# Attention and mixture of experts on one core: turning and first products of the normalised rows in halves of 64

## The chip, the cores and the metric

The kernel runs on one core of a Trainium2 chip. The metric is the device time in microseconds, as the median of several runs; a profiled execution gives one more time and a trace. The engines are named PE (matrix products and transposes), PEld (PE's loading of the stationary operand, which can overlap its products), DVE (vector), ACT (scalar), POOL and SP (which here starts most transfers).

## The reference, cut to what matters

```python
x = L0_attn_x                          # (2, 4096, 512) float32
xn = _layernorm(x, axis=-1)
x = x + attention(xn) + moe(xn)

# attention: causal, 64 wide, from a compressed row
c = (xn @ W_to_kv.T) @ W_compress.T    # 64 wide; then a layernorm, q, k, v, rope, softmax, output
# moe: 16 experts, 2 per token, and a shared one
router_logits = xn @ router_w.T        # 16 wide; softmax, top 2
shared = (silu(xn @ shared_gate_w) * (xn @ shared_up_w)) @ shared_down_w
```

All arithmetic is in float32. There are 8192 tokens of width 512. The change concerns how `xn` is transposed and how the 16 router logits and the 64 compressed values of each token are computed from the transposed rows.

## The kernel before, in words

The work has three phases. The first goes through 16 groups of 512 tokens (the list `seq`, which alternates between the two sequences of the batch): normalise, transpose, router logits and compressed values, the shared expert, and after every second group the projection to q, k and v. The second runs attention in part and the routed experts, the third the rest of attention with the sums of all parts. Only the first phase is touched. The second and third have their order on PE, DVE and ACT written out by hand (from L863); in the first phase the order on each engine is set by a scheduler when the kernel is built, which follows the program's order, but lets a later instruction pass an earlier one that isn't ready.

A group's steps, in program order:

- `front` (L341) makes `xn` from the rows `xt`: statistics on DVE, a root on ACT, four scalings on DVE (L350). It is called through `ahead()` (L436) in the middle of the group before, so the next `xn` is there early. Then POOL adds the output bias to `xt` (L353); the group's results are added to `xt` later.
- `group` (L397) transposes `xn` into `xnT`: for each of four column blocks `c`, four transposes of 128 x 128 (L402) into a bank of pool B, and one copy to `xnT`, three on ACT and one on DVE (L403).
- `plc` (L404 to L409): for each of four row blocks `i`, four products over `c` with `RC`, the router and compressing weights side by side (80 columns), summed in one bank, O. In the trace each float32 product is two passes, each with its own weight load. DVE copies the logits to `lg` (L411), takes statistics of the 64 compressed values (L415, L416), scales them into `cn` (L420), and finds the top two experts (L425, L426). The two weights go into two extra columns of `xn`, which SP stores to `xn_d` (L437).
- The shared expert's gate and up products, `gu` (L306, called by `product`), are a seven-product scheme of quarters of the matrices: `moved` (L286) makes sums of quarters of `xnT` on DVE, in place for one of them; each product fills a pair of banks of pool A and is taken into sums by ACT or DVE (L471 to L488).
- The down product, `pd`, has seven products too, in the order 1, 2, 4, 6, 7, 5, 3. Their banks alternate (L513): 1, 6 and 3 in T, 2 and 5 in O, 4 and 7 in half of a pair of A. DVE adds each to `xt` (`onto_x`, L521). The last lines are quoted below. SP stores `xt` to `acc_d` (L540).
- After each group of the second sequence, `project` (L546) transposes `cn` into a B bank (`ptc`), scales it into `chT` on DVE, and computes q and k (`qk`, two A pairs, L560; DVE multiplies by the rope table, L562; POOL adds, L563) and v (`pv`, an A pair, L568). Its products have 64 summands, with the two sequences in the two halves of the partitions.

PSUM has eight banks here: A two pairs, B two, O one and T one.

```python
                c5 = summed(5)
                V.tensor_tensor(m2, m2, c5, ALU.add)
                onto_x(1, 1, c5)
                onto_x(1, 1, m3)
                onto_x(1, 0, m3)
                onto_x(0, 1, summed(3))
                onto_x(0, 1, m2)
```

Of the kernel before, what the change touches and what calls it, by code (L numbers as in the profile page):

```python
# [8 lines left out]
F32 = mybir.dt.float32  # L9
# [3 lines left out]
ALU = mybir.AluOpType  # L13
# [6 lines left out]
P = 128  # L20
# [8 lines left out]
DC = 64  # L29
NE, FE, FS = 16, 256, 512  # L30
# [22 lines left out]
def tile_mla_then_moe(  # L53
# [23 lines left out]
    mm, tr = nc.tensor.matmul, nc.tensor.transpose  # L77
    V, S, G = nc.vector, nc.scalar, nc.gpsimd
# [13 lines left out]
    def psA(name):  # L92
        return ps.tile([P, 2, 512], F32, tag="A", name=name)

    def psB(name):
        return ps.tile([P, 512], F32, tag="B", name=name)

    def psO(name, second=False):
        return ps.tile([P, 512], F32, tag="T" if second else "O", name=name, bufs=1)
# [3 lines left out]
    def kept(shape, dtype, name):  # L103
        return keep.tile(shape, dtype, tag=name, name=name)


    ident = kept([P, P], F32, "ident")
# [167 lines left out]
    def quarter(t, i, j):  # L275
        return t[:, 2 * i:2 * i + 2, j * 256:(j + 1) * 256]
# [23 lines left out]
    def product(pieces, n):  # L300

        for o, fac in pieces:
            lhs, rhs = fac[n]
            for r in range(2):
                for c in range(2):
                    mm(out=o[:, r, :], lhsT=lhs[:, c, r * P:(r + 1) * P], rhs=rhs[:, c, :],  # L306
                       start=c == 0, stop=c == 1)


    with tc.tile_pool(name="p1w", bufs=1) as pw:  # L310
        gam = pw.tile([P, 1], F32, name="gam")
        bet = pw.tile([P, 1], F32, name="bet")
        RC = pw.tile([P, 4, NE + DC], F32, name="RC")
# [9 lines left out]
        with tc.tile_pool(name="p1", bufs=2) as p1:  # L323
# [11 lines left out]
            def rstd_of(mv, n, name):  # L335
                r = p1.tile([P, n], F32, tag="rstd", name=name, bufs=4)
                S.activation(r, mv[:, :, 1], AF.Sqrt, bias=eps_t)
                V.reciprocal(r, r)
                return r

            def front(g, xt):  # L341
                st = p1.tile([P, 4, 6], F32, tag="st", name=f"st{g}")
                mv = p1.tile([P, 4, 2], F32, tag="mv", name=f"mv{g}")
                for i in range(4):
                    V.bn_stats(st[:, i, :], xt[:, i, :])
                    V.bn_aggr(mv[:, i, :], st[:, i, :])
                r = rstd_of(mv, 4, f"rx{g}")
                xn = p1.tile([P, 4, D + TOPK], F32, tag="xn", name=f"xn{g}", bufs=1)
                for i in range(4):
                    V.tensor_scalar(xn[:, i, 0:D], xt[:, i, :], mv[:, i, 0:1], r[:, i:i + 1],  # L350
                                    ALU.subtract, ALU.mult)

                G.tensor_tensor(xt, xt, b_bc.unsqueeze(1).to_broadcast([P, 4, D]), ALU.add)  # L353
                return (xn,)
# [3 lines left out]
            def rank_of(g, idx8):  # L358
# [35 lines left out]
                            in_=tok[:, g * 4 + i, k:k + 1], in_offset=None)  # L394
                ranked.append(scatter)

            def group(g, xt, xn, cn, ahead):  # L397
                xnT = p1.tile([P, 4, 512], F32, tag="xnT", name=f"xnT{g}", bufs=1)
                for c in range(4):
                    pt = psB(f"pt{g}_{c}")  # L400
                    for i in range(4):
                        tr(pt[:, i * P:(i + 1) * P], xn[:, i, c * P:(c + 1) * P], ident)  # L402
                    (V.tensor_copy if c == 3 else S.copy)(xnT[:, c, :], pt)  # L403
                plc = psO(f"plc{g}")  # L404
                lc = plc.rearrange("p (i f) -> p i f", f=P)
                for i in range(4):
                    for c in range(4):
                        mm(out=lc[:, i, 0:NE + DC], lhsT=xnT[:, c, i * P:(i + 1) * P], rhs=RC[:, c, :],
                           start=(c == 0), stop=(c == 3))  # L409
                lg = p1.tile([P, 4, NE], F32, tag="lg", name=f"lg{g}")  # L410
                V.tensor_copy(lg, lc[:, :, 0:NE])  # L411
                st = p1.tile([P, 4, 6], F32, tag="st", name=f"stc{g}")
                mv = p1.tile([P, 4, 2], F32, tag="mv", name=f"mvc{g}")
                for i in range(4):
# [9 lines left out]
                for i in range(4):  # L424
# [11 lines left out]
                nxt = ahead()  # L436
                nc.sync.dma_start(  # L437
                    out=xn_d[g * 512:(g + 1) * 512, :].rearrange("(i p) d -> p i d", p=P), in_=xn
# [77 lines left out]
                def summed(n):  # L516
                    t = banks[n](f"pd{n}_{g}").rearrange("p (r d) -> p r d", r=2)
                    product([(t, fac_d)], n)
                    return t

                def onto_x(i, j, t):  # L521
                    xq = quarter(xt, i, j)
                    V.tensor_tensor(xq, xq, t, ALU.add)
# [11 lines left out]
                onto_x(1, 1, c5)  # L535
                onto_x(1, 1, m3)
                onto_x(1, 0, m3)
                onto_x(0, 1, summed(3))
                onto_x(0, 1, m2)
                nc.sync.dma_start(  # L540
                    out=acc_d[g * 512:(g + 1) * 512, :].rearrange("(i p) d -> p i d", p=P), in_=xt
# [30 lines left out]
            seq = [b * GPB + h for h in range(GPB) for b in range(NB)]  # L572
# [30 lines left out]
            pt = psB("pt_rw")  # L603
# [3 lines left out]
            pt = psB("pt_wcm")  # L607
            tr(pt[:, 0:DC], wcm, ident[:DC, :DC])
            V.tensor_copy(wcmT, pt[:, 0:DC])
            pt = psB("pt_wc")  # L610
            for c in range(4):
                mm(out=pt[:, c * DC:(c + 1) * DC], lhsT=wtk[:, c * P:(c + 1) * P], rhs=wcmT,
                   start=True, stop=True)
# [27 lines left out]
                    nc.sync.dma_start(out=order_d[t].rearrange("(p f) o -> p (f o)", p=P), in_=kc_z)  # L641

            cur = (x_first, *front(seq[0], x_first))
            cn = None
            for n, g in enumerate(seq):

                def ahead(n=n):
                    if n + 1 == len(seq):
                        return None
                    t = load_x(seq[n + 1])  # L650
                    return (t, *front(seq[n + 1], t))

                if g < GPB:
                    cn = p1.tile([P, 4, NB, DC], F32, tag="cn", name=f"cn{g}")
                cur = group(g, *cur, cn, ahead)
                if g >= GPB and g != seq[-1]:
                    project(g - GPB, cn)
                while ranked:
                    ranked.pop()()
# [507 lines left out]
```

## Time and profile before

| what | us |
|---|---|
| median of 3 runs | 2021.14 (2018.82 to 2023.4) |
| profiled execution | 1979.99 |
| its span | 1977.8 |
| PE busy in the span | 1898.8 (96%) |
| DVE busy | 1073.7 (54%) |
| ACT busy | 626.8 (32%) |
| transposes of `xn`, L402, in PE time | 40.2 (x256) |
| `plc`, L408, in PE time | 64.6 (x512 passes) |

The time of the profiled execution is its span and 2.2 us around it. It is one execution; the runs of the median are others. Busy times of PE are the sum of overlapping passes as the profile models them, so what a pass costs is read from the distance between starts, not from its duration: a merged group's length, less one duration, over the number of steps between. In a timeline, "x8" is eight merged instructions, and the bracket is the idle time of the engine before them and who ended it. "128*64 64x128"-like entries give rows times columns of the array, then the operand's partitions and elements.

### The profile page before, as it was taken

The page shows a single profiled execution, that of the slowest core. Times are in us where ns is not written, and L with a number is a line of the kernel's source. Part 1 is how long each engine was busy: PE and PEld are TensorE (multiplying, and loading weights), DVE is VectorE, ACT ScalarE, POOL GpSimd, SP SyncE. Part 2 cuts the span into 40 slices and gives each one's busy share as a digit, 9 for nine tenths or more (in the row PEclk, how much of TensorE's full clock was granted, in tenths as well). Part 3 has the DMA queues.
Part 4 walks back from the last instruction along what each step waited for, and adds up shares of the span by engine and source line. Part 5 has one row for each costly group of instructions (what it writes and reads, how often), then busy time and mean ns, then how long its engine had stood idle before and what let it go on. Part 6 is the DMA issues. An engine that isn't in the chain of part 4 may idle for free. (4 is left out here: it accounts for less than half of the span.)

```text
span 1977.8 us, 31805 instructions
## 1 busy us (share of the span) xinstructions
PE 1898.8 (96%) x12210; PEld 1407.1 (71%) x12210; DVE 1073.7 (54%) x2910; ACT 626.8 (32%) x1045; POOL 572.0 (29%) x499
## 2 busy tenths in 40 slices
PE   7999999999999988899999999999999999999997
PEld 6888888888888865467777777777777675444453
DVE  8878777787778766632222222222222324777775
ACT  2222222223222213541111111111111355576663
POOL 2333333323233341111111111111111104555554
PEclk9999999999999988999999999999999999999998
DMA  6122222222222213138788887877887776888887
GB/s 233 65 76 65 75 86 76 97 86 75 64 75 65 75 43 123 33 102 278 250 279 282 272 276 264 293 270 264 277 279 245 245 240 187 208 200 212 200 207 181
DMA packets 219434, 342.40 MB, mean 173 GB/s; under 512 B 19204, under 2 KB 109952, under 8 KB 219280
## 3 DMA queue, kind: packets, MB, share of 16 engines
q1 hardware_dynamic: 167600, 234.09, 36.4%
q0 software_dynamic: 31696, 69.99, 14.1%
q10 hardware_dynamic: 19984, 36.25, 4.8%
q8 instruction: 98, 1.61, 0.3%
q14 instruction: 56, 0.46, 0.1%
HBM read 250.22 MB, written 90.05 MB: 172 GB/s over the span
## 5 line engine op out<-in xcount | busy, mean ns | idle before, releaser
L995 PE MATMUL pg<-xt,wgu 128*128 128x256 f32 (+1 forms) x2816 | 496.1, 335 | 0.0
L995 PEld LDWEIGHTS pg<-xt,wgu 128*128 128x128 f32 x2816 | 434.8, 191 | 43.0 <-issue 0.5
L917 POOL DMA_INDIRECT xg<-xn_d,table x137 | 130.8, 955 | 685.5 <-DVE sw L977 553.0
L1001 DVE TENSOR_TENSOR eh<-esg,pg 128x512 f32<-128x512 f32 (+1 forms) x69 | 47.2, 684 | 396.6 <-ACT esg L1000 396.6
L1009 PE MATMUL py<-wdn,eh 128*128 128x512 f32 x548 | 247.1, 594 | 0.0
L972 DVE COPY xt<-pxt 128x512 f32<-128x512 f32 x138 | 88.3, 682 | 176.7 <-PE pxt L969 176.5
L1009 PEld LDWEIGHTS py<-wdn,eh 128*128 128x128 f32 x548 | 102.2, 190 | 106.6 <-issue 98.5
L742 ACT ACTIVATE E<-E,nb 128x1024 f32<-128x1024 f32 (+7 forms) x160 | 160.4, 1004 | 42.0 <-DVE nb L737 39.4
L1013 ACT ACTIVATE y<-py,sw 128x512 f32<-128x512 f32 x137 | 94.2, 688 | 231.1 <-PE py L1009 200.2
L734 DVE TENSOR_SCALAR_CACHE_REDUCE E<-s 128x512 f32<-128x512 f32 x224 | 143.5, 686 | 43.3 <-PE s L726 32.4
L1000 ACT ACTIVATE esg<-pg 128x512 f32<-128x512 f32 (+1 forms) x69 | 41.0, 594 | 382.8 <-PE pg L995 322.7
L726 PE MATMUL s<-kT,qT 64*128 64x512 f32 (+3 forms) x576 | 143.2, 595 | 11.4 <-DVE E L734 7.3
L392 POOL DMA_INDIRECT order_d<-tok,at_u x128 | 129.3, 1010 | 64.4 <-issue 36.4
L796 PE MATMUL oT<-eT,vv 128*64 128x256 f32 x1088 | 146.2, 391 | 0.4 <-DVE eT L782 0.2
L776 PEld LDWEIGHTS et<-ident,E 64*128 64x128 f32 x2112 | 81.7, 141 | 81.6 <-issue 50.1
L782 ACT COPY eT<-et 128x512 f32<-128x512 f32 x186 | 102.1, 586 | 102.9 <-PE et L776 66.3
L796 PEld LDWEIGHTS oT<-eT,vv 128*64 128x64 f32 x1088 | 67.3, 138 | 91.6 <-issue 35.3
L776 PE MATMUL et<-ident,E 64*128 64x64 f32 x2112 | 103.9, 233 | 26.0 <-ACT eT L782 15.4
L1084 POOL DMA_INDIRECT fac<-y_d,pos_all x64 | 98.8, 1544 | 71.3 <-DMA fac<-y_d,pos_all 56.4
L353 POOL TENSOR_TENSOR x<-x,b_bc 128x2048 f32<-128x2048 f32 x16 | 76.1, 4754 | 147.3 <-DVE xn L350 134.6
L1084 POOL DMA_INDIRECT fyy<-y_d,pos_all x64 | 82.7, 1292 | 114.0 <-ACT eT L782 54.2
L306 PE MATMUL gu<-xnT,Wg 128*128 128x256 f32 x384 | 98.5, 391 | 6.3 <-DVE ft L185 3.3
(241 smaller groups left out, 2782.4 us busy)
## 6 DMA issues: line engine op xcount, KB each, us to landing
wgu<-in_L_ffn_gate_w_dram SPq DMA_DIRECT2D x88, 512.0 KB, 6.0
wgu<-in_L_ffn_up_w_dram SPq DMA_DIRECT2D x88, 512.0 KB, 8.5
wdn<-in_L_ffn_down_w_dram SPq DMA_DIRECT2D x88, 512.0 KB, 4.1
y_d<-y ACTq DMA_DIRECT2D x137, 256.0 KB, 6.2
xn_d<-xn SPq DMA_DIRECT2D x16, 1028.0 KB, 4.9
x<-in_L_attn_x_dram SPq DMA_DIRECT2D x16, 1024.0 KB, 6.6
acc_d<-x SPq DMA_DIRECT2D x16, 1024.0 KB, 5.2
fac<-acc_d SPq DMA_DIRECT2D x64, 256.0 KB, 4.9
```

The lines of the kernel that those rows point to most:

```text
L306: mm(out=o[:, r, :], lhsT=lhs[:, c, r * P:(r + 1) * P], rhs=rhs[:, c, :], start=c == 0, stop=c == 1)
L392: G.indirect_dma_start(out=order_d[n % 4], out_offset=bass.IndirectOffsetOnAxis(ap=at_u[:, i, k:k + 1], axis=0), in_=tok[:, g * 4 + i, k:k ...
L726: mm(out=sc[b][:, 0:w], lhsT=q[e, :], rhs=kT[c][e, 0:w], start=True, stop=True)
L734: V.tensor_scalar(dst, sc[b][:, 0:w], SCALE, None, ALU.mult, ALU.max, accum_out=m)
L742: S.activation(E, E, AF.Exp, bias=nb[:, b:b + 1], accum_out=sm[:, b, c:c + 1])
L776: tr(pt[h][:, o:o + H], rows[i][j // 8][e, b, (j % 8) * P:(j % 8 + 1) * P], ident[e, e])
L782: copy(dst[:, h:h + 3:2, :], pt[h].rearrange("p (u c) -> p u c", u=2))
L796: mm(out=o, lhsT=vv[j // 4][:, b, j % 4, :], rhs=e, start=(j == 0), stop=(j == n - 1))
L917: G.indirect_dma_start(out=x_n, out_offset=None, in_=xn_d, in_offset=bass.IndirectOffsetOnAxis(ap=table[:, n:n + 1], axis=0))
L995: mm(out=pg[:, g, f, at_s], lhsT=weights[u][0][:, c, g * FE + f * P:g * FE + (f + 1) * P], rhs=x_u[:, c, :], start=(c == 0), stop=(c == 3))
L1009: mm(out=py[:, v, :], lhsT=hT[:, c, v * P:(v + 1) * P], rhs=weights[u][1][:, c, :], start=(c == 0), stop=(c == 1))
L1084: G.indirect_dma_start(out=y, out_offset=None, in_=y_d, in_offset=bass.IndirectOffsetOnAxis(ap=pos[k][:, j:j + 1], axis=0), compute_op=ALU ...
```

## The change

A new function `turn_x` transposes the next group's `xn`. It is called in `group` just ahead of the last down product (`pd3`), and once ahead of the loop. Each 128-row transpose becomes two of 64 rows, one per half `h` of the partitions, and each half has its own bank: two banks of B for the first two column blocks, one pair of A for the other two. Four copies, all on ACT, put the halves side by side in `xnT`.

The products with `RC` are split over the summands: partitions 0 to 63 into bank O, 64 to 127 into bank T, alternating. ACT copies the first bank to `lc0`, DVE adds the second to it into `lc`, in SBUF. The logits are a view of `lc`; statistics and scaling read `lc` where they read the bank.

```diff
+            turned = {}
+
+            def turn_x(g, xn):
+                xnT = p1.tile([P, 4, 512], F32, tag="xnT", name=f"xnT{g}", bufs=1)
+                for c2 in (0, 2):
+                    if c2:
+                        pair = psA(f"pt{g}_{c2}")
+                        pt = [pair[:, h, :] for h in range(2)]
+                    else:
+                        pt = [psB(f"pt{g}_{c2}_{h}") for h in range(2)]
+                    pt = [t.rearrange("p (c i q) -> p c i q", c=2, i=4) for t in pt]
+                    for c in range(2):
+                        for i in range(4):
+                            for h in range(2):
+                                e = slice(h * 64, (h + 1) * 64)
+                                tr(pt[h][:, c, i, :], xn[e, i, (c2 + c) * P:(c2 + c + 1) * P], ident[e, e])
+                    for h in range(2):
+                        S.copy(xnT[:, c2:c2 + 2, :].rearrange("p c (i h q) -> p c i h q", i=4, h=2)[:, :, :, h, :], pt[h])
+                turned[g] = xnT
+
             def group(g, xt, xn, cn, ahead):
-                xnT = p1.tile([P, 4, 512], F32, tag="xnT", name=f"xnT{g}", bufs=1)
-                for c in range(4):
-                    pt = psB(f"pt{g}_{c}")
-                    for i in range(4):
-                        tr(pt[:, i * P:(i + 1) * P], xn[:, i, c * P:(c + 1) * P], ident)
-                    (V.tensor_copy if c == 3 else S.copy)(xnT[:, c, :], pt)
-                plc = psO(f"plc{g}")
-                lc = plc.rearrange("p (i f) -> p i f", f=P)
+                xnT = turned.pop(g)
+                pl = [psO(f"plc{g}_{h}", h == 1).rearrange("p (i f) -> p i f", f=P) for h in range(2)]
                 for i in range(4):
                     for c in range(4):
-                        mm(out=lc[:, i, 0:NE + DC], lhsT=xnT[:, c, i * P:(i + 1) * P], rhs=RC[:, c, :],
-                           start=(c == 0), stop=(c == 3))
-                lg = p1.tile([P, 4, NE], F32, tag="lg", name=f"lg{g}")
-                V.tensor_copy(lg, lc[:, :, 0:NE])
+                        for h in range(2):
+                            e = slice(h * 64, (h + 1) * 64)
+                            mm(out=pl[h][:, i, 0:NE + DC], lhsT=xnT[e, c, i * P:(i + 1) * P], rhs=RC[e, c, :],
+                               start=(c == 0), stop=(c == 3))
+                lc0 = p1.tile([P, 4, NE + DC], F32, tag="lc0", name=f"lc0{g}", bufs=1)
+                lc = p1.tile([P, 4, NE + DC], F32, tag="lc", name=f"lc{g}", bufs=1)
+                S.copy(lc0, pl[0][:, :, 0:NE + DC])
+                V.tensor_tensor(lc, lc0, pl[1][:, :, 0:NE + DC], ALU.add)
+                lg = lc[:, :, 0:NE]
...
                 onto_x(1, 0, m3)
+                if nxt is not None:
+                    turn_x(seq[seq.index(g) + 1], nxt[1])
                 onto_x(0, 1, summed(3))
...
             cur = (x_first, *front(seq[0], x_first))
+            turn_x(seq[0], cur[1])
```

## The prediction

> **What bounds the kernel now.** I first read the busy times by stretch, since the change lives in the first phase only (it ends near 745 us; the weights of the last `gu` products that read `xnT` are loaded at 751.7 us). The columns are stretch, length, then busy time (and count) of PE, PE's weight loads, DVE, ACT, POOL, the granted clock and DMA.
>
> ```profile
> core 0: us, PE busy (x) PEld busy (x) DVE busy (x) ACT busy (x) POOL busy (x), PEclk, DMA share, GB/s
> ...
> 200.00:300.00 100.00, 98.49 (x540) 83.55 (x537) 76.27 (x191) 27.82 (x38) 34.76 (x30) 1.00 0.27 86
> 300.00:400.00 100.00, 98.79 (x526) 85.71 (x526) 79.62 (x227) 29.30 (x41) 30.71 (x26) 1.00 0.24 79
> ```
>
> PE is busy 98 to 99% at full clock; DVE follows at 76 to 80%, ACT has room (29%), DMA too. So a microsecond less on PE counts, as long as DVE keeps up. The matching waits of PE itself from 60 to 700 us name hardly anything but the transposes waiting for their banks (`PE pt L402 <- ACT xnT L403`, 6.4 us in 14 waits). "Busy" hides more than that, though, because matmul ends are modelled; so next I read PE's weight loads in order of time (start, duration from first to last of the merged group), at a group boundary with no projection, which is 8 of the 16:
>
> ```profile
> 335.21 1.70 PEld L306 LDWEIGHTS pd<-Wd,hs 128*128 128x128 f32 x8
> 336.94 1.01 PEld L402 LDWEIGHTS pt<-ident,xn 128*128 128x128 f32 x8
> 338.43 0.42 PEld L402 LDWEIGHTS pt<-ident,xn 128*128 128x128 f32 x4 [0.48 <-ACT xnT L403]
> 338.81 0.30 PEld L408 LDWEIGHTS plc<-RC,xnT 128*128 128x128 f32 x2
> 338.99 0.47 PEld L402 LDWEIGHTS pt<-ident,xn 128*128 128x128 f32 x4
> 339.43 0.62 PEld L408 LDWEIGHTS plc<-RC,xnT 128*128 128x128 f32 x4
> 339.98 0.73 PEld L306 LDWEIGHTS gu<-xnT,Wg 128*128 128x128 f32 x4
> 340.74 3.09 PEld L408 LDWEIGHTS plc<-RC,xnT 128*128 128x128 f32 x26
> 343.74 0.73 PEld L306 LDWEIGHTS gu<-xnT,Wg 128*128 128x128 f32 x4
> ```
>
> Three things are in it. The stretch from the first transpose to the `gu` after the last `plc` is 343.74 - 336.94 = 6.80 us, of which four `gu` passes are other work (8 passes take 1.72 us: 0.86 us), so transposes and `plc` cost **5.94 us**. A `plc` pass costs (3.09 - 0.19)/25 = 0.116 us; 80 columns are fewer than the loads need. And PE's order isn't program order: `gu` overtakes a `plc` whose `xnT` is late, but no `plc` of a later `i` does, so products into one bank stay in order while another tile may pass.
>
> At the 7 boundaries with a projection, loads run from `ptc` at 379.48 to the `gu` after `plc` at 392.83: 13.35 us, less six `gu` passes (1.30) = **12.05 us**. Its work: `ptc` 0.55, 16 transposes at 0.11 = 1.75, `qk` eight pairs at 0.43 = 3.43, `pv` 1.04, `plc` 32 x 0.113 = 3.6; together 10.4. About 1.65 us is waiting, mostly for `chT` (DVE) and for the transposes' banks.
>
> **Price of half rows.** Two shapes already in the trace stand in for the new ones. Transposes of 64 rows, a bank per half (L969), and fp32 products with 64 summands, halves alternating between two banks (L568, the projection of v):
>
> ```profile
> 1211.29 1.02 PE L1009 MATMUL py<-wdn,eh 128*128 128x512 f32 x2
> 1212.24 0.57 PEld L969 LDWEIGHTS pxt<-ident,xg 64*128 64x128 f32 x16 [0.76 <-issue]
> ...
> 1212.88 0.41 PEld L995 LDWEIGHTS pg<-xt,wgu 128*128 128x128 f32 x3
> ```
> ```profile
> 385.46 0.97 PEld L568 LDWEIGHTS pv<-WvT,chT 64*128 64x128 f32 x16 [0.81 <-DVE ro L562]
> ...
> 386.50 0.20 PEld L402 LDWEIGHTS pt<-ident,xn 128*128 128x128 f32 x2
> ```
>
> A half transpose costs (0.57 - 0.138)/15 = 0.029 us; a half product pass (0.97 - 0.188)/15 = 0.052 us. The new `plc` pass has 80 moving columns where `pv` has 64. In proportion to the 256 columns of `gu` (0.215) 80 take 0.067, less than the 0.104 at which each half gets its turn, so I keep 0.052; the upper end is 0.065 (grown with the columns), which would cost 0.8 us a group.
>
> Here two rules of the Trainium skill speak against the change. *TensorE: Matmul & The Clock Gate*, "LDWEIGHTS", says load time goes by columns and not by rows. The row agrees for one load: 182 to 188 ns for 64 rows, 186 to 192 ns for 128. By that rule alone, 64 loads at 0.113 would take 7.2 us; by the spacing of `pv` 64 x 0.052 = 3.33 us. The trace decides, but only for halves that *alternate*; a half running alone is priced by the rule. *TensorEngine Tiling (Array Packing)*, "Key Properties", says a changed tiling mode drains the array. The trace puts a number on it: the last full `py` pass streams till about 1212.15 (second of two starting 0.43 apart, 0.43 long), the next full load is at 1212.88, so 0.73 us for 16 x 0.029 = 0.46: **0.27 us a visit** (`pv`: 1.04 - 0.83 = 0.21). Without the drain the change would be worth some 9 us more over 15 boundaries.
>
> **The change, part by part** (all against the profiled execution: 1979.99 us, of which 1977.8 are span).
>
> *Transposes.* 16 full ones go, 32 halves come: 32 x 0.029 + 0.27 = 1.20 us, and they stand ahead of the last down product, with banks that have long been free (B: only `prk` used it; the A pair is that of `pd4`, read at 331.5, while the turn starts near 335.6). No wait: `xn` is ready at about 315. Their four ACT copies (4 x 0.59) run beside the 1.73 us of the last down product; ACT does nothing else there. If that cover failed, the second pair of copies would hold `plc` for about 0.2 us.
>
> *DVE.* One `xnT` copy (0.69) and `lg` (0.22) go; the 320-wide add comes (between 0.42 at 256 and 0.69 at 512: 0.48). A net 0.4 us less; counted as nothing, since DVE isn't the bound. The ACT copy `lc0` (about 0.42, by ACT's 0.37 at 256 and 0.59 at 512) lengthens the path from `plc` to `bn_stats` by some 0.5 us. DVE works 0.9 to 2 us ahead of the banks that PE needs (L479 ends at 320.26, `gu3` starts at 321.17), so that too is nothing, or 0.5 us a group if the cover is gone. Behind `lc` on DVE queue the top-8 steps, the weights in `xn`, the next `bn_stats`; SP's `xn_d` store waits for the weights and moves with them. POOL and the SP queue are otherwise untouched.
>
> *`plc` in halves.* 64 x 0.052 + 0.27 = 3.60 us. A new wait: the second bank is T, and the last down product `pd3` is in T. It is read by DVE `onto_x(0,1,pd3)`: start 0.04 us after the product's end (as L534 at 335.63 after 335.59), 0.68 long, 0.05 to PE, so T is free 0.77 after. Half loads could begin 0.07 before that end (as L969), so the wait is 0.84. Whether PE waits, or first half `plc` runs alone for seven passes and the second catches up alone, it is the same: 14 x (0.113 - 0.052) = 0.85. Between 0 (if `gu` fills it) and 1.15 (if no load is prefetched); I take 0.84, because the scheduler's order puts first-half `plc` before `gu`.
>
> *Sum without projection:* 1.20 + 3.60 + 0.84 = 5.64 against 5.94: 0.3 us saved, x 8 = 2.4 us. *With projection:* 1.20 + `ptc` 0.55 + `plc` 3.33 + five pairs alone 0.57 + `qk` 3.43 + `pv` 0.83 + three mode changes at 0.2 = 10.5 against 12.05: 1.5 us saved, x 7 = 10.7. Here the waits go: in the 2 us until `chT` is there, `plc` is ready and no transpose waits for a copy. Next late would be `ro` (DVE, POOL), which holds `gu`'s banks until about 8 us after `pd3`; `plc` lasts until 8.7. The first group, where PE waits on DVE anyway, I put at 0.5. Together **13.6 us**: 1979.99 becomes 1966.4, a ratio of 0.9931; on the median, 2021.14 x 0.9931 = **2007 us** (its runs are 2% longer than the profiled one; I scale).
>
> **Rivals.**
> *Better (0.20): the T wait is filled.* If `gu` takes it (it already overtakes `plc` above) and the projection's waits go whole, boundaries save 1.1 and 2.2: 8.8 + 15.4 + 1 = 25 us, 1995. For it: the reordering; against: first-half `plc` stands ahead of `gu`.
> *No difference (0.20): given back, on DVE.* The longer path through ACT shifts `bn_stats`, the weights and the next `xn` by 0.5 to 0.7 us; if that eats the 0.9 us that DVE is ahead, 15 x 0.7 = 10 us are given back: 2018. For it: DVE at 80%; against: DVE has 0.4 us less to do.
> *Slower (0.18): halves that don't pair.* The order on PE is fixed when the kernel is built. If T is judged free late, many first halves run in a row, then as many second halves, each load at 0.113. A pair run apart costs 0.122 more; my gain is 0.9 a group, so from about 8 pairs more than those counted, of 32, the change loses. At 16 pairs apart: about 2025; all 32: (25 x 0.122 - 0.9) x 15 = 32 us, 2053. For it: T is indeed taken to the last moment; against: the wait is 0.8 us, seven passes.
> The upper end of the half pass, 0.065, would by itself take 12 us and land on the second rival. That the halves don't overlap at all even when alternating is excluded by `pv`.
>
> **How the numbers follow.** Main case 0.42: 2007, own range 2001 to 2014. With the rivals at 1995, 2018 and 2025 to 2053, the range that leaves out 2 in 10 is 1994 to 2027. About 0.2% (4 us) is what a measurement can tell from no change. Faster: 0.42 + 0.20 = 0.62; same 0.20; slower 0.18.
>
> **What would show it.** Two groups (one of each kind) take 91.2 us now (`plc` x26 at 340.74 and 431.94); 89.4 expected, 91 would be the DVE rival, above 91.5 the pairing one. Transposes 0.03 apart in one run before the last `pd`; `plc` loads 0.05 apart after a wait of under 1 us for `x` L523, or in runs 0.11 apart if one half goes alone. DVE waits before `bn_stats` for ACT's `lc0`. I am wrong if PE waits for banks in `gu` (DVE late), if each mode change costs more than 0.5 us, or if later phases don't shift by what the first one saves.

## The result, and the profile after

The changed kernel took 2119.47 us (2116.3 to 2121.28, 4 runs) where the kernel before took 2020.75 (2018.82 to 2023.4): a ratio of 1.0468, 95% interval 1.0433 to 1.0503. Its profiled execution took 2118.56 us, of which 2116.4 are span. Forecast were 2007, range 1994 to 2027.

Runs were taken in sets, side by side with the kernel before, and the sets fall in two kinds, **prompt** ones in which the kernel before takes 1984 to 1986 us as a median, and **late** ones in which it takes 2020 to 2039; this result and the three runs on which the forecast was scaled are late, the trace from which it was worked out (1979.99 us) is prompt, and a ratio is always one within a set.

The first phase ended at about 880 us instead of 750. The busy times by stretch, columns as before (length, PE, PEld, DVE, ACT, POOL, clock, DMA), for the same stretches:

```profile
core 0: us, PE busy (x) PEld busy (x) DVE busy (x) ACT busy (x) POOL busy (x), PEclk, DMA share, GB/s
200.00:300.00 100.00, 91.33 (x534) 76.97 (x533) 65.83 (x173) 24.61 (x36) 30.30 (x26) 0.90 0.20 67
300.00:400.00 100.00, 91.34 (x545) 77.25 (x543) 65.84 (x148) 21.84 (x32) 29.98 (x25) 0.93 0.14 51
```

Two things are lost at once: PE is busy 91% instead of 98 to 99, and the granted clock is 0.90 to 0.93 instead of 1.00. Two groups take 109.1 us instead of 91.2 (first copies of the turn at 330.99 and 440.07). PE's weight loads at a boundary without projection, in order of time:

```profile
167.64 1.09 PEld L414 LDWEIGHTS pt<-ident,xn 64*128 64x128 f32 x32 [0.33 <-issue]
168.79 1.59 PEld L306 LDWEIGHTS pd<-Wd,hs 128*128 128x128 f32 x8
170.72 0.52 PEld L427 LDWEIGHTS plc<-RC,xnT 64*128 64x128 f32 x4 [0.33 <-issue]
175.94 7.83 PEld L427 LDWEIGHTS plc<-RC,xnT 64*128 64x128 f32 x60 [4.70 <-ACT xnT L416]
183.92 2.21 PEld L306 LDWEIGHTS gu<-xnT,Wg 128*128 128x128 f32 x6
```

The 32 half transposes are as cheap as forecast (1.09 us). Then PE stands for 4.70 us, because ACT's copies of the second pair of banks are late; and after this pause 60 half products take 7.83 us, at half clock. ACT, the same moment:

```profile
169.09 1.07 ACT L416 COPY xnT<-pt 128x512 f32<-128x512 f32 x2 [9.33 <-PE pt L414]
174.82 1.07 ACT L416 COPY xnT<-pt 128x512 f32<-128x512 f32 x2 [4.65 <-remote]
```

The transposes for the second copy ended at 168.87 and PE's signal of it came at 174.79, where such a signal elsewhere in the first phase follows 0.014 us (the median) behind the modelled end. "remote" is how the profile names a releaser that it can't place. DVE waits the same way for the last down product (`DVE x L545 <- remote`, 69.7 us in 14 waits). The clock's record shows half clock for 6.8 us after one sort of group and 13.7 after the other: 10.2 on average (it is recorded in steps of 3.4), which costs up to 5.1; some of it falls into the pause. PE stands for 4.1 to 4.7 us at each of fourteen boundaries (1.6 at the first), and with the half clock this makes the 9 us a group that the two groups show (17.9 / 2). Fourteen times 9 is 126 us, and that is by how much the first phase is longer than in the trace before (last `pd` load at 890.1 instead of 763.9). The other 12 of the 139 us between the two spans are lost later.

POOL at that time issues the eight indirect DMAs that write the group's ranks to `order_d` (L392), one each 1.28 us:

```profile
163.43 0.99 POOL L392 DMA_INDIRECT order_d<-tok,at_u  x1 [1.89 <-DVE at_u L387]
...
171.19 0.97 POOL L392 DMA_INDIRECT order_d<-tok,at_u  x1 [0.30 <-issue]
172.46 0.97 POOL L392 DMA_INDIRECT order_d<-tok,at_u  x1 [0.30 <-issue]
```

These eight in a row are called the burst below.

### The profile page after: what moved, and what is told of

Read it like the earlier page. It is cut to its first block, busy times and chain, and to the rows that moved or that the text cites. A ratio compares the mean times of both kernels' runs of the same rounds, so it can differ in the third digit from the quotient of the medians.

```text
span 2116.4 us, 33374 instructions
## 1 busy us (share of the span) xinstructions
PE 1977.4 (93%) x12978; PEld 1462.2 (69%) x12978; DVE 1066.4 (50%) x2894; ACT 644.0 (30%) x1077; POOL 567.4 (27%) x499
## 5 line engine op out<-in xcount | busy, mean ns | idle before, releaser
L427 PE MATMUL plc<-RC,xnT 64*128 64x80 f32 x1024 | 116.7, 364 | 63.0 <-ACT xnT L416 61.4
L427 PEld LDWEIGHTS plc<-RC,xnT 64*128 64x128 f32 x1024 | 109.0, 267 | 75.7 <-ACT xnT L416 63.7
L392 POOL DMA_INDIRECT order_d<-tok,at_u x128 | 126.4, 987 | 64.4 <-issue 36.7
L1109 POOL DMA_INDIRECT fac<-y_d,pos_all x64 | 98.7, 1542 | 73.7 <-DMA fac<-y_d,pos_all 59.0
```

The lines of the kernel that those rows point to most:

```text
L392: G.indirect_dma_start(out=order_d[n % 4], out_offset=bass.IndirectOffsetOnAxis(ap=at_u[:, i, k:k + 1], axis=0), in_=tok[:, g * 4 + i, k:k ...
L427: mm(out=pl[h][:, i, 0:NE + DC], lhsT=xnT[e, c, i * P:(i + 1) * P], rhs=RC[e, c, :], start=(c == 0), stop=(c == 3))
L1109: G.indirect_dma_start(out=y, out_offset=None, in_=y_d, in_offset=bass.IndirectOffsetOnAxis(ap=pos[k][:, j:j + 1], axis=0), compute_op=ALU ...
```

## The experiments

**First round: theories about PE's own order.** A stall is the wait of PE at the turn, with its late signal, that the profile after shows. The first theory (A): half-row transposes followed by a full product hold back the signals. Its rivals: first-half products running alone (B), the A pair of the second transposes (C); then, when these had failed, a half product alone behind a full one (D), any order half, full, half (E), the wait for T, and PE standing at a copy that waits for PE's own signal. Each run changes one of these (edits against the changed kernel, except where said).

*Turn behind the last down product.*
```diff
-                if nxt is not None:
-                    turn_x(seq[seq.index(g) + 1], nxt[1])
                 onto_x(0, 1, summed(3))
                 onto_x(0, 1, m2)
+                if nxt is not None:
+                    turn_x(seq[seq.index(g) + 1], nxt[1])
```


> The changed kernel with the turn placed behind the last down product, so that half-row transposes are followed by half-row products and no full product stands between. Theory A (the signal that the half-row transposes are done comes late when a full-row product follows them): no copy waits over 1 us behind its transposes, clock near 0.99, time within 1% of the kernel before. Theory B (the first-half plc products, run alone and then blocked, hold the signals back): the stall of 4.65 us a group stays, time near 2119 us. Theory C (a copy is late because of the pair of A banks): stall stays.

Measured: 1995.05 us, before 1985.87, ratio 1.0039 (1.0017 to 1.0062). No stall.

*Whole rows turned ahead, products in halves.*
```diff
...
-                                tr(pt[h][:, c, i, :], xn[e, i, (c2 + c) * P:(c2 + c + 1) * P], ident[e, e])
...
+                        tr(pt[:, i * P:(i + 1) * P], xn[:, i, c * P:(c + 1) * P], ident)
...
```


> The turn ahead of the last down product, but with full-row transposes; plc in halves as in the changed kernel. Theory A: no stall behind the transposes, time within 1.5% of the kernel before. Theory B: the stall stays, near 2119 us. Theory C: stays.

Measured: 1986.86, ratio 1.0016 (1.0000 to 1.0033). No stall.

*Halves turned ahead, products whole.*
```diff
-                        for h in range(2):
...
-                            mm(out=pl[h][:, i, 0:NE + DC], lhsT=xnT[e, c, i * P:(i + 1) * P], rhs=RC[e, c, :],
...
+                        mm(out=lc[:, i, 0:NE + DC], lhsT=xnT[:, c, i * P:(i + 1) * P], rhs=RC[:, c, :],
...
```


> Half-row transposes ahead of the last down product, plc in full rows in one bank as before. Theory A: the stall of about 4.65 us a group stays, time near 2110 us. Theory B: no stall, time within 1% of the kernel before. Theory C: stays.

Measured: 1973.72, ratio 0.9951 (0.9922 to 0.9980). No stall.

*Old turn in its old place, products in halves.* The transposes are those of the kernel before, the rest is the change.

> Full-row transposes in their old place, only plc in halves. Theories A and C: no stall of over 1.5 us; the time shows the price of the plc part alone, by my prediction's terms a loss or gain of under 1 us a group: 2010 to 2035 us. Theory B: where a first half runs alone and PE then waits, a stall of some us stays, above 2060 us.

Measured: 2008.76 (two runs), ratio 1.0120 (1.0075 to 1.0165). No stall.

*Second half of the products in a B bank instead of T.*
```diff
-                pl = [psO(f"plc{g}_{h}", h == 1).rearrange("p (i f) -> p i f", f=P) for h in range(2)]
+                pl = [(psB if h else psO)(f"plc{g}_{h}").rearrange("p (i f) -> p i f", f=P) for h in range(2)]
```


> The changed kernel, with the second half of plc in a B bank, so that it need not wait for the reading of the last down product in T; the two halves then alternate from the first product on. Theory D (the turn's signals are held only when one half of plc runs alone behind the full-row down product): no stall, clock 0.99, near the kernel before (within 1%). Theory E (held whenever half-row transposes, a full-row product and half-row products follow one another): the stall of some 4.65 us a group stays, about 5% slower.

Measured: 1977.21, before 1984.84, ratio 0.9965 (0.9949 to 0.9981). No stall; the halves alternate, 64 loads in 3.65 us.

*Whole products, with two first-half products ahead of them into a B bank that nobody reads* (extra work).

> The fast variant (half-row turn ahead of the last down product, plc in full rows) plus two products of the first half rows alone, into a B bank that nobody reads, between the down product and plc; extra work, the output is unchanged. Their own price is 4 passes of 0.11 us and two mode changes, about 1 us a group, 15 us. Theory D: the stall comes back, about 5% slower than before. Theory E: it comes back too. Theory F (the stall needs the wait for the T bank or for the last product's reader): no stall, within 1% of before.

Measured: 1987.19, ratio 1.0012 (1.0001 to 1.0023). No stall.

*Turn one down product earlier, ahead of `c5 = summed(5)`.*

> The changed kernel with the turn ahead of the last but one down product, so that two full-row products stand between it and plc and the four copies have 3.5 us. Theory D and E: the signals are still held, stall of some us a group, over 2% slower than before. Theory G (signals are late only because PE is blocked on a copy that itself waits for them): no stall, since PE isn't blocked on a copy, within 1% of before.

Measured: 1985.47, ratio 1.0011 (0.9990 to 1.0031). No stall.

All seven ran in prompt sets, and none stalled. So either every one of these parts is needed, or the stall has nothing to do with them. The kernel itself had to be run again beside them:

> The changed kernel itself, unaltered, on the chip of the other three runs. If the held completion signals belong to the program: 1.03 to 1.055 of before, and in its trace ACT L416 and DVE L545 wait for 'remote' 4 to 5.5 us a group again, clock about 0.95. If they belonged to the one chip or moment of the first run: about 0.997 to 1.003, and no such wait.

Measured: the same changed kernel took **1979.42 us**, before 1983.81: ratio 0.9972 (0.9962 to 0.9982). No late signal at all. Every theory of the first round falls with it; they had explained a difference between sets by differences between kernels. PE's weight loads of this run at a boundary without projection:

```profile
338.26 1.08 PEld L414 LDWEIGHTS pt<-ident,xn 64*128 64x128 f32 x32 [0.33 <-issue]
339.40 1.59 PEld L306 LDWEIGHTS pd<-Wd,hs 128*128 128x128 f32 x8
341.33 4.61 PEld L427 LDWEIGHTS plc<-RC,xnT 64*128 64x128 f32 x64 [0.33 <-ACT xnT L416]
346.01 1.59 PEld L306 LDWEIGHTS gu<-xnT,Wg 128*128 128x128 f32 x8
```

Beside it ran three more. *As the second half in B, but the whole first half written ahead of the second* (the loop over `h` outermost, and nothing else is different from f1):

> Second half of the products in a B bank instead of T (as the run that was free of the stall), but the whole first half is written ahead of the second, so that first-half products run alone behind the last down product and PE then stands at the copy of the second pair of transposes, with no wait for T. Theory 'one half alone while PE waits for a copy whose transposes lie behind a full product': stall of 4 to 5 us a group, 1.03 to 1.05. Theory 'wait for T is needed': no stall; 64 products at 0.072 to 0.113 instead of 0.055, so 1 to 3.5 us a group more than with alternating halves, 1.005 to 1.025 of before, clock about 0.99. If the chip decides: same as the latter.

Measured: 2066.25, ratio 1.0392 (1.0354 to 1.0429). That is the number of the first theory, but not for its reason: no signal is late and PE never stands. The second theory, which had no stall either, allowed no more than 1.025. The cost is another one. Stretches, and PE's loads there:

```profile
334.00:336.00 2.00, 2.00 (x24) 2.00 (x23) 0.05 (x1) 1.45 (x2) 1.27 (x1) 1.00 0.48 79
336.00:338.00 2.00, 2.00 (x17) 1.86 (x15) 0.69 (x1) 0.26 (x1) 0.00 (x0) 0.82 1.02 388
338.00:340.00 2.00, 2.00 (x5) 1.64 (x6) 1.90 (x18) 0.39 (x2) 0.00 (x0) 0.50 0.74 287
```
```profile
332.92 4.82 PEld L427 LDWEIGHTS plc<-RC,xnT 64*128 64x128 f32 x44
337.89 2.95 PEld L306 LDWEIGHTS gu<-xnT,Wg 128*128 128x128 f32 x8
```

Halves that run alone take 0.11 us each, and behind some 5 us of them the clock is 0.50 although PE was busy throughout: the next eight `gu` loads take 2.95 us instead of 1.70. The clock's record has such a stretch, mostly of 3.4 to 10.2 us, in every group. In f1, where the same halves alternate, the mean clock is 0.990; here it is 0.964. So a half product alone is paid for twice.

*Last down product in an A bank, so that no product waits for T.*
```diff
-                         7: lambda n: psA(n)[:, 0], 5: psO, 3: lambda n: psO(n, True)}
+                         7: lambda n: psA(n)[:, 0], 5: psO, 3: lambda n: psA(n)[:, 0]}
```


> The changed kernel with the last down product in an A bank instead of T; so no product waits for T and the halves alternate from the first pair, in O and T as in the change. If the stall needs the wait for T or a half alone: no stall, 0.993 to 0.999 of before, as with the second half in B. If it needs the bank T for products or anything else that stays here: stall again, 1.03 to 1.05.

Measured: 1977.49, ratio 0.9965 (0.9950 to 0.9980). No stall; but the unaltered kernel didn't stall in this set either, so it decides nothing about T.

*Halves turned ahead, products whole, again.*

> The best version so far (turn in halves of 64 ahead of the last down product, router and compressing products whole, in O), beside the changed kernel on one chip. 0.992 to 0.998 of before; no stall, clock 0.99. If the first result was the chip's own state, it would here lie with the changed kernel within 0.5%.

Measured: 1972.41, ratio 0.9937 (0.9915 to 0.9959); the best in a prompt set, as at first.

**Second round: what is late in a late set.** Three kernels were traced in one set, which turned out late (before 2034.85 us).

> The kernel before, traced beside the changed kernel. Theory 'the chip holds completion signals': on a chip where before takes about 2020 us, its trace too has some 40 us of waits for 'remote' in ACT or DVE, or half clock, behind pieces of half-row work (8 projections of 5 us each would be 40); theory 'only the changed order stalls': before loses its 35 us elsewhere (DMA, clock) and no wait for 'remote'. On a chip where before takes about 1985 us: neither.

> The changed kernel on a further chip. If the chip decides: 2110 to 2125 where before takes about 2020, 1975 to 1985 where before takes about 1985. If chance decides from run to run: either, whatever before takes.

> Half-row turn ahead of the last down product, router and compressing products whole. Where before takes about 1985: 1967 to 1979. Where before takes about 2020: about 2006 if the stall needs products in halves of 64 behind a full product, 2090 or more if half-row transposes alone bring it.

Measured, one run each: the kernel before 2031.75, the changed one 2116.86 with the stall at fourteen boundaries again, halves turned with whole products 2056.97 with a stall at seven, between the two values expected. So the kind of set decides, and half-row products are not needed. The chip alone doesn't decide: the record gives the same chip number, 3, for this late set and for the prompt one of f1, f3 and f5, 20 minutes earlier. The kernel before has late signals too, at its seven boundaries without projection; its waits of DVE, and the copy at one of them:

```profile
DVE xnT L403 <- remote: 25.2, 7, 3.9
```
```profile
161.23 0.97 POOL L392 DMA_INDIRECT order_d<-tok,at_u  x1 [0.31 <-issue]
163.63 0.69 DVE L403 COPY xnT<-pt 128x512 f32<-128x512 f32 x1 [3.78 <-remote]
```

Its first phase ends 38 us later than in the prompt trace (last `pd` load at 802.5 instead of 764.1): most of its extra time (51.8 us of span) is there, and no line of the trace shown before could tell of it. In each of these stalls POOL's burst of L392 was under way. The late copy starts 2.3 to 2.5 us after the start of the burst's last issue at 41 of the 42 late boundaries of the four late traces (after, h1, h2, h3): in the kernel before as above (163.63 after 161.23), in h2 so:

```profile
169.80 0.97 POOL L392 DMA_INDIRECT order_d<-tok,at_u  x1 [0.31 <-issue]
172.30 1.07 ACT L416 COPY xnT<-pt 128x512 f32<-128x512 f32 x2 [3.29 <-remote]
```

It doesn't follow the burst's packets: in h2 the last of them mostly start 0.75 us before the copy, in h1 0.3 to 3.3 us after it. That gave the next theory: in a late set PE's completion signals are held while the burst runs.

**Third round: the burst moved.** *The changed kernel with POOL's burst held back into the next group*, by indices that DVE writes there from a sum of the gate and up products. Two small DVE instructions a group are added:
```diff
+                        V.tensor_scalar(z, late, 0.0, None, ALU.mult)
+                        V.tensor_scalar(at_u, at_f, z, None, ALU.add)
...
                 V.tensor_tensor(k2, k2, b5, ALU.add)
+                if ranked:
+                    ranked.pop()(k2[:, 0, 0:1])
...
-                while ranked:
-                    ranked.pop()()
```


> The changed kernel with POOL's eight indirect DMAs of a group (L392) held back to the middle of the next group's gate and up products, by indices that DVE writes there (two small DVE instructions more a group). Theory 'PE's completion signals are held while POOL's burst of indirect DMAs runs', on a chip where before takes 2020 us or more: no wait for 'remote' at the turn, 1985 to 2025, that is 0.99 or less of before. Theory 'the burst has nothing to do with it': 2105 to 2120 there, 1.04 of before, waits for 'remote' of 4 to 5 us a group at L416 as now. Where before takes about 1985 there is no stall to remove: 1977 to 1987 under both.

Measured, before 2039.04 and so late: **2022.52**, ratio 0.9915 (0.9882 to 0.9948). No wait for "remote" at the turn is left in the first phase; the slowdown of 4.0 to 4.7% in the two late sets that had the changed kernel became a gain. One group tests the theory within the run. The last has no next group, so the edit issues the bursts of the last two groups there, beside its `plc`, and there the signal is late: `plc` ends at 735.07, and DVE gets it 2.0 us after the burst's last issue.

```profile
734.63 0.44 PE L432 MATMUL plc<-RC,xnT 64*128 64x80 f32 x2 [0.18 <-issue]
736.39 0.97 POOL L397 DMA_INDIRECT order_d<-tok,at_u  x1 [0.30 <-issue]
738.38 0.69 DVE L292 TENSOR_TENSOR xnT<-xnT 128x512 f32<-128x512 f32 x1 [5.03 <-remote]
```

What remains elsewhere is a wait that the edit made: DVE's next ranks need POOL, which is still in the burst, and PE waits for DVE behind them, 2.5 us at seven boundaries:

```profile
PE pd L306 <- DVE x L554: 17.3, 7, 2.5
```

*The same with halves turned and whole products.*

> Half-row turn ahead of the last down product, router and compressing products whole, and POOL's eight indirect DMAs held back in the same way. Theory of the burst, where before takes 2020 or more: the seven stalls of 5 us with their half clock go, 1970 to 1995, 0.98 of before or less; otherwise about 2055, 1.01. Where before takes about 1985: 1967 to 1980, 0.992 to 0.998.

Measured: 2041.10, ratio 1.0004 (0.9985 to 1.0024). The stalls at the turn went, but the same self-made wait is longer here (`PE pd L306 <- DVE hs L534`, 41.3 us in 7 waits), so the expected 0.98 was missed. Hence a third placing, at the first sum of the next group, where POOL has nothing to do:
```diff
                 S.copy(k1, sent(1))
+                if ranked:
+                    ranked.pop()(k1[:, 0, 0:1])
```


> Half-row turn ahead of the last down product, router and compressing products whole, POOL's eight indirect DMAs held back to the first gate and up product of the next group, that is before and not between POOL's own work for the next ranks. Theory of the burst: neither stall nor the wait for ranks of the later placement; where before takes 2020 or more, 1980 to 2005 (0.970 to 0.985); where before takes about 1985, 1965 to 1980 (0.991 to 0.998). If the burst merely carries its stall with it into the gate and up products: 2035 or more on the former.

> The kernel before with the same placing of the eight indirect DMAs and nothing of the change. Theory of the burst: where before takes 2020 or more, its own late signals at seven boundaries go (some 25 us of waits and half clock), 1990 to 2015, 0.98 to 0.99 of before, and j1 stays 0.4 to 0.8% under it. Where before takes about 1985: 0.998 to 1.003.

Measured, before 2037.57 and so late: halves turned with whole products **1990.98**, ratio 0.9772 (0.9740 to 0.9803); the kernel before with nothing but this placing 2002.02, ratio 0.9825 (0.9797 to 0.9853). Both came as the theory of the burst said. But the theory is too wide: beside `gu` neither trace has a wait for "remote". In j1, in the middle of a burst, DVE starts 0.04 us behind the end of the product that it adds (224.84 + 1.89):

```profile
224.84 1.89 PE L306 MATMUL gu<-xnT,Wu 128*128 128x256 f32 x8
226.75 0.97 POOL L396 DMA_INDIRECT order_d<-tok,at_u  x1 [0.30 <-issue]
226.77 1.22 DVE L503 TENSOR_TENSOR gs<-gs,gu 128x1024 f32<-128x1024 f32 x1 [1.98 <-issue]
```

Stretches of 300 to 400 us of the former and of the latter:

```profile
300.00:400.00 100.00, 98.59 (x554) 84.59 (x553) 84.45 (x232) 31.29 (x43) 31.21 (x28) 1.00 0.26 90
```
```profile
300.00:400.00 100.00, 97.31 (x524) 83.66 (x524) 80.16 (x203) 26.78 (x37) 31.66 (x27) 1.00 0.24 85
```

Full clock and a busy PE in a late set: the placing alone is worth 1.75%, and the half-row turn, made ahead of the last down product, 0.55% on top (1990.98 / 2002.02 = 0.9945; by the two intervals about 0.004 either way).

## Why the prediction was wrong, point by point

- **The step that failed** is in the turn's cost: "No wait", and the four copies that "run beside the 1.73 us of the last down product"; if that failed, `plc` was to wait "about 0.2 us". It waited 4.1 to 4.7 us at fourteen boundaries, and half clock after it cost about as much again. The cover holds only if PE's signals come, and in the late sets those of the second transposes and of the last down product came 4 to 6 us late. "POOL and the SP queue are otherwise untouched" was true of their work; I didn't ask what POOL was doing at the turn. The burst was in the trace before: its issues start from 331.3 to 340.3 us, around the boundary that I quoted. So the kernel before turns inside the burst too, but in h1 its PE has `gu` passes to put in while the last copy is late and stands only 1.1 to 2.0 us, at seven boundaries. The changed one has four `plc` passes (and `ptc`, where there is a projection), and what comes next in its order needs the second pair of copies.
- **The scaling failed too.** "Its runs are 2% longer than the profiled one; I scale" took an unexplained 41 us for a uniform stretch, though the runs agree within 0.12% of their median. It was, as far as the late trace h1 tells, mostly a stall at the very boundary under change: 25 us of waits, and half clock. It doesn't scale; it grew from seven boundaries to fourteen.
- **The rival for slower** ("halves that don't pair", 2025 to 2053) named another mechanism. In part it was right: in g0 the first half does run ahead alone for 16 of 63 steps, and in g1, where it runs alone for long, it costs 4%. It is not what took 2119.
- **The sum, in a prompt set, where its conditions hold.** Forecast 0.9931, measured 0.9972: a gain of 4.4 us (1983.81 less 1979.42) for 13.6. Two groups take 90.65 us (copies at 339.00 and 429.65) where 91.2 were and 89.4 expected.
  - Half transposes: 1.08 us for 32, (1.08 - 0.138)/31 = 0.030, as expected (0.029). With the changes of mode the turn costs 1.44 us, not 1.20: PE's loads idle for 0.33 us before it, where 0.27 for the whole visit was counted.
  - `plc` without projection: from the end of the last down product to `gu` 4.88 us, not 4.44. Of this, 3.93 (337.27 to 341.20 in f1, which doesn't need T) stand for the 3.60 of the products, with 0.33 us of idle again; the other 0.95 for the 0.84 of T. PE doesn't stand for T: the first half runs alone for 16 steps, as one of the two readings in the forecast had it (14). The boundary costs 6.32 us, against 5.94 before: 0.4 more instead of 0.3 less.
  - With projection: from 379.42 to 393.73 less 16 `pd` passes at 0.216, 10.9 us, against 12.05 before and 10.5 forecast. This gain, 1.2 us for 1.5, was nearly right in size.
  - 8 x 0.7 and 7 x 0.4 account for some 8 of the 9.2 us missing.
- **The price of a half product** was about right: (3.65 - 0.19)/63 = 0.055 us where halves alternate throughout (f1), forecast 0.052. By the rule on loads that I weighed a load would have taken 0.113; it holds where halves run alone (0.11 in g1), not where they alternate. What I didn't draw from my own sum is that the split saves nothing: 64 halves take 3.65 us where 32 whole ones take 3.76 (e3), and two changes of mode, an ACT copy and a DVE add come on top. Whole products behind the new turn are at 0.9937 to 0.9951, the change at 0.9972, halves with the old turn at 1.0120. So the gain was in the turn, none in the split products. Most of it may lie in the place and not in the half rows: with halves as products, whole rows turned ahead (e2) are at 1.0016, in the old place (e4) at 1.0120. Whole rows turned ahead with whole products were not run.
- "Later phases don't shift" was named as a sign of being wrong. They do shift, and lose the 12 us named above, 8 of them in the third phase: at its start POOL issues a burst as well (L1109), and ACT, in code that the change doesn't touch, waits in the profile after:

```profile
1789.87 1.07 ACT L807 COPY eT<-et 128x512 f32<-128x512 f32 x2 [7.57 <-remote]
```

**What stays open.** That the stall of a late set needs the burst at the turn is shown by moving it (i1, i3, j1, j2), by the last group of i1, and by the copies that start 2.3 to 2.5 us after its last issue. How the burst holds signals is not shown, nor why it holds those at the turn and not those of `gu` (j1) or of the down products in its first half (in the profile after, the one that ends at 167.71 is signalled at 167.73). What makes a set late isn't known: the kernel and its instructions are the same. It isn't the burst's pace (1.28 us an issue in both kinds), and no delay of its packets tells the kinds apart: in the kernel before the last ones start 2.0 to 5.9 us after the last issue in the prompt trace and 2.2 to 5.8 in the late one. Moving the burst doesn't make a late set prompt: j1 and j2 still take 18 us more than the same kernels without the placing in prompt sets (1990.98 against 1972.41, 2002.02 against 1983.81), and where these go wasn't followed. Nor did these runs settle why the kernel before and the whole products escape at boundaries with projection. The trace suggests, and no run shows, that PE has `ptc` and `qk` to do there while the signals are late.

## What to carry to other kernels

When the runs of a kernel are longer than its trace by more than they differ among themselves, the trace may be of another condition: find the missing microseconds before you build on it, and run the changed kernel again beside the experiments before explaining its slowness by its edit. When a step is moved, look at every engine at the place where it lands, the one that only issues DMAs too: a burst of indirect DMAs beside a chain PE, ACT, PE with no slack cost 9 us a group here in late sets, and the same burst beside the long first products of the next group no stall at all. Splitting products into halves of 64 rows saved nothing even alternating, and running alone for 5 us they brought the clock down to 0.50.

## What the runs showed of the hardware that was not expected

- PE's completion signals came 3 to 6 us late in some sets, while its products kept their pace in the record, and the copies that waited for them started 2.3 to 2.5 us after the last issue of POOL's burst of indirect DMAs.
- The granted clock fell to 0.50 behind 5 us of half-row products alone, with PE busy 100% of the time.
- Around a pause of PE of 4.1 to 4.7 us the clock stayed at half for 6.8 to 13.7 us; of the 9 us that this cost a group, the half clock took about as much as the pause.
